# Four preln graph-attention layers on one core: the first group's query and key products made plainly and by halves, and the values of layer 3's last two groups made last

## The chip, the cores and the metric

One core of one Trainium2 chip runs the kernel. The metric is device microseconds of one execution, as the median of several; the trace shows one profiled execution. TensorE is called PE in the profile, VectorE DVE, ScalarE ACT and GpSimd POOL; SP is the engine that issues most of the DMAs, and "SPq" and "ACTq" are DMA issues on the queues of SP and ACT.

## The reference

The input is 128 graphs of 64 nodes with 512 features (8192 rows) and a 64x64 adjacency for each graph. Four layers follow, each on `h = relu(layernorm(x))` and added to `x`. All is float32. Cut to what matters:

```python
# layers 0 and 2: 4 heads of 64
q, k, v = h @ Wq, h @ Wk, h @ Wv
attn = softmax(where(adj, q @ k.T / 8, -max))
x = x + (attn @ v) @ Wo + bo
# layer 1: a second layernorm, 8 heads, the same attention with qkv and out projections
# layer 3: 8 heads
m = h @ map_w.T + map_b
n = m / norm(m per head)
cos_adj = (n @ n.T masked > 0.1)
q, k = m @ q_w.T + q_b, m @ k_w.T + k_b
adj_h = cos_adj * softmax(where(mask, NEG, q @ k.T / 8)) * keep
sem = h @ gcn_map_w.T + gcn_map_b            # the "values" of this layer
out = relu((adj_h @ sem) @ gcn_W.T / (adj_h.sum(-1) + 1))
x = x + out
```

## The kernel before

**Tiling.** The rows go in 16 groups of 512 rows (8 graphs), and the layers one after the other: group 0 to 15 of layer 0, then layer 1, and so on. A step is a pair (layer, group). For each step the rows are loaded in two halves of 256 rows (L468, on SP's queue), normalised (statistics on DVE at L433 to L438 and L442, a power on POOL at L440, the scaling on ACT at L449), transposed by PE (L500) and copied by ACT into `hT` (L505).

**Products.** A product of 512 rows with a 512x512 weight is done by a Strassen-Winograd scheme (`winograd`, L539): 7 products of quarters where a plain one has 8. Each product of quarters is 4 float32 matmuls, which the profile counts as 8 passes (`x8`). The price is sums: four of the weight's quarters, once for each weight (`sums_of_a`, L315, on POOL; kept in blocks 2, 4, 5 and 6 of the weight tile, block 2 being overwritten) and four of the input's quarters for each step (`sums_of_b`, L327, on POOL, into a tile `t`). The PSUM evictions of a product are ACT's and DVE's (L552, L556, L565, L572, L576 and, for the values of layer 3, L638 to L659). The values of layers 0 and 2 are plain products (L682, `mmv`).

**Layer 3.** For a group, `m` is made first (`map3`); then, up to group 14, the values `S2` (`sem3`, tile `v` in the profile), then q and k. In group 15 q and k come before the values. POOL adds a bias row to the values (`add_rows`, L780, four instructions), and `norms` (L791 to L827) scales `m` to unit length by way of a DRAM round trip (L811, L819, on SP's queue).

**Softmax and the end of a group.** `front` does for each half of a group's blocks (u = 0, 1): scores (L847, 64 small matmuls into the PSUM tile `sc`, of which there is one, shared with `po`), mask, maximum, subtraction (L858, L863, L866, DVE), exponential (L869, ACT), sum and reciprocal (L872, L874), scaling (L876, POOL); in layer 3 also the cosine scores from `m`, their threshold (L1108) and the mask product (L1114). The tile `E` comes from a ring of two. `last` (layer 3) transposes E (L887, copied by ACT at L891), multiplies with the values (L1141, `po`), and `finish` divides (L1052, L1054, L1057) and adds the residual (L1063). The residual rows are loaded by 16 DMAs for a group (L1042) and the result stored by 16 (L1070), all on SP's queue, and the ring `xres` of the residual tiles holds two, that is one group.

**What sets the order.** The order of the instructions on each engine is decided when the kernel is built: `Order` runs generators with estimated durations, and each one's next instruction is put down when its engine is free in that estimate. Weight loads count 10 us each there, but those that follow each other on the queue overlap, and the last one counted for `vo0` is the 2 us of `bo0`. On the chip each engine takes its instructions in that order and waits at each for what it needs. `weights` (L333 to L351) loads the weights one after the other on ACT's queue and yields the POOL sums between them:

```python
            w_ready[key].set()
            yield from sums_of_a(o_part(t) if key in ("vo0", "vo2") else t)
            w_sums[key].set()
```

Of the kernel before, what the change touches and what calls it, by code (L numbers as in the profile page):

```python
# [16 lines left out]
N = 64  # L17
# [186 lines left out]
def gnn_stack(ctx: ExitStack, tc: tile.TileContext, a: dict, out: bass.AP):  # L204
# [85 lines left out]
    def o_part(t):  # L290

        return t.rearrange("p a k n -> p (a k) n")[:, 4:11, None, :]
# [24 lines left out]
    def sums_of_b(B, T, vector=False):  # L317

        n = T.shape[2]
        for o, i0, i1 in ((T[:, 0], B(0, 1), B(0, 0)), (T[:, 1], B(1, 1), T[:, 0]),  # L320
# [4 lines left out]
            else:  # L325
                yield pool(0.65 * n)
                nc.gpsimd.tensor_tensor(o, i0, i1, ALU.subtract)  # L327

    def weights():
        for key, parts in units:  # L330
            if key == "q1":
                yield p_ready[0, 0]
            t, w_done[key] = yield from r_w.new(f"w_{key}")  # L333
            W[key] = t
            for src, dst in parts(t):
                yield ("actq", 1.0, 10.0)
                nc.scalar.dma_start(dst, src.rearrange("(c p) o -> p c o", p=P))
            if key in ("vo0", "o1", "vo2"):
                l = int(key[-1])
                src = a[f"bo{l}"]  # L340
                bo[l], bo_done[l] = yield from r_u.new(f"bo{l}")
                yield ("actq", 0.5, 2.0)
                nc.scalar.dma_start(bo[l], bass.AP(tensor=src.tensor, offset=src.offset,
                                                   ap=[[0, P], [1, D]]))
            if key in ("q1", "k1", "v1"):
                yield from gamma_into(key)
            elif key == "o1":
                yield from v_bias()
            elif key == "sem3":
                yield from gcn_fold(t)  # L350
            w_ready[key].set()  # L351
            yield from sums_of_a(o_part(t) if key in ("vo0", "vo2") else t)
            w_sums[key].set()

    bv = const.tile([P, NC], F32, name="bv")

# [93 lines left out]
                                 scale=rs[:, 0, t:t + 1])  # L450

    hT, hB, h_ready, h_done, t_done = {}, {}, {}, {}, {}

    def quarters(v):

# [32 lines left out]
    def transposes(steps):  # L488

        for l, s in steps:  # L490
            h, h_done[l, s] = yield from r_h.new("hT")
            hT[l, s] = h
            for half in range(2):
                yield n_ready[l, s, half]
                x, xe = normed.pop((l, s, half))
                for t in range(2):
                    pt, pe_ = yield from r_tr.new("ptr")
                    for c in range(NC):
                        yield pe(0.115)
                        nc.tensor.transpose(pt[:, c, :], x[:, t, c * P:(c + 1) * P], ident)  # L500
# [12 lines left out]
            yield from sums_of_b(quarters(h), T)  # L513
            sums.set()
# [67 lines left out]
    def winograd(A, BT, tokens_out, out_, used, begun):  # L582
# [102 lines left out]

    st, p_ready, s_ready, p_used, with_ones = {}, {}, {}, {}, []

    def projections(steps):
        for l, s in steps:
            yield h_ready[l, s]  # L690
            h, BT = hT[l, s], hB[l, s]
            z = st[l, s] = {}
            end = s == NG - 1
            if l in (0, 2):
                yield w_ready[f"qk{l}"]
                qk, z["qk_done"] = yield from r_qk.new("qk")
                used = yield from unit(W[f"qk{l}"], (*BT, w_sums[f"qk{l}"]), False, Out(quarters(qk)))
                od.spawn(when([used], s_ready[l, s], t_done[l, s],
                              w_done[f"qk{l}"] if end else None), 0)
                z["q"], z["k"] = qk[:, 0:2, :], qk[:, 2:4, :]  # L700
                yield w_ready[f"vo{l}"]
# [8 lines left out]
            elif l == 1:  # L710
                es = []
                for i, n in enumerate("qk"):
                    yield w_ready[f"{n}1"]
                    o, z[f"{n}_done"] = yield from r_qk.new(f"{n}T")
                    es.append((yield from unit(W[f"{n}1"], (*BT, w_sums[f"{n}1"]), False,
                                               Out(quarters(o), qkb[:, i, :]))))
                    od.spawn(when([es[-1]], w_done[f"{n}1"] if end else None), 0)
                    z[n] = o
                od.spawn(when(es[:2], s_ready[l, s]), 0)
                yield w_ready["v1"]  # L720
                V, z["v_done"] = yield from r_v.new("V")

                def vv(i, k, V=V):
                    return V[:, 2 * k:2 * k + 2, i * H:(i + 1) * H]
                es.append((yield from unit(W["v1"], (*BT, w_sums["v1"]), True, Out(vv))))
                z["v"] = V
                od.spawn(when(es, p_ready[l, s], t_done[l, s], h_done[l, s],
                              w_done["v1"] if end else None), 0)
            else:
                yield w_ready["map3"]  # L730
                mT, z["m_done"] = yield from r_m.new("mT")
                mv = quarters(mT)
                m_ready = yield from unit(W["map3"], (*BT, w_sums["map3"]), False, Out(mv, map_b))
                m_sums, z["n_ready"], m_used = od.event(), od.event(), od.event()
                od.spawn(sums_after(m_ready, mv, z, m_sums), 1)
                od.spawn(norms(mT, s, m_ready, z["n_ready"], m_used), 3)
                order = ("q", "k", "sem") if end else ("sem", "q", "k")
                es, rows = [], od.event()
                for n in order:
                    yield w_ready[f"{n}3"]  # L740
                    if n == "sem":
                        V, z["v_done"] = yield from r_v.new("S2")
                        S2 = V.rearrange("p t (h e) -> p t h e", e=N + 1)
                        if not any(V is v for v in with_ones):

                            with_ones.append(V)
                            yield pool(0.6)
                            nc.gpsimd.memset(S2[:, :, :, N:N + 1], 1.0)

                        def sv(i, k, S2=S2):  # L750
                            return S2[:, 2 * k:2 * k + 2, 4 * i:4 * i + 4, 0:N]
                        used = yield from unit(W["sem3"], (*BT, w_sums["sem3"]), True, Heads(sv))
                        od.spawn(when([m_ready, used], t_done[l, s], h_done[l, s]), 0)
                        od.spawn(add_rows(S2, used, rows), 0)
                        z["v"] = S2
# [12 lines left out]
    def sums_after(e, B, z, done):  # L768
        yield e
# [81 lines left out]
    def softmax_parts(S, se, mask, neg):  # L851

        m = mask.rearrange("p b k -> p (b k)")
        n = m.shape[1]
# [9 lines left out]
        E, e = yield from r_e.new("E")  # L864
# [12 lines left out]
        return E, e  # L877

    def transposed(E, e):

# [197 lines left out]
    def front(l, s):  # L1078
# [6 lines left out]
            z["e_ready", u] = od.event()  # L1085
        p_used[l, s].set()
        for u, blocks in enumerate(units):
            S, se = yield from scores(z["q"], z["k"], 2 * nch, blocks)
# [5 lines left out]
            E, e = yield from softmax_parts(S, se, m, (0, 1, 0, 2)[l])  # L1094
            if u == len(units) - 1:
                me.set()
            z["e", u] = E, e
# [22 lines left out]
    def last(s):  # L1120
# [102 lines left out]
```

## Time and profile before

| | |
|---|---|
| median of 6 runs | 3003.63 us (3000.38 to 3010.83) |
| profiled execution, its own time | 3004.57 us |
| its span in the profile | 3002.8 us |
| busy PE / DVE / ACT / POOL | 98% / 58% / 45% / 50% of the span |
| mean granted TensorE clock | 0.992 |
| DMA moved | 244.08 MB, 81 GB/s on average |

The page divides the span by engine, then into 40 slices, then lists DMA queues, the chain of work that ended last, and the costliest groups of instructions. A line of the timeline gives start, duration, engine, line, operation, and output and input tiles; what stands in brackets is the engine's idle time before it and what ended it. "The profile's own time" is 1.8 us above the span.

### The profile page before, as it was taken

To read this page: it belongs to the slowest core of one execution; us is meant where nothing else is said; L and a number is where in the kernel's file an instruction comes from. 1 tells how busy PE (TensorE), PEld (TensorE's weight loads), DVE (VectorE), ACT (ScalarE), POOL (GpSimd) and SP (SyncE) were. 2 spreads that over 40 slices of the span, in tenths; PEclk is the share of its full clock that TensorE was granted. 3 is DMA by queue.
4 is the path that set the end of the run, shared out by engine and by line. 5 is a ranking of instruction groups with operands and counts; after the bars stand their busy time and mean duration, and the time that the engine had idled before them with its cause. 6 is when DMAs were issued, how large, how long until landed. Compare 5 with 4: busy or idle time off the path is not lost.

```text
span 3002.8 us, 64290 instructions
## 1 busy us (share of the span) xinstructions
PE 2935.3 (98%) x27288; PEld 2490.5 (83%) x27288; DVE 1747.3 (58%) x2753; ACT 1358.4 (45%) x2489; POOL 1493.7 (50%) x1168
## 2 busy tenths in 40 slices
PE   8999999999999999999999999999999999999997
PEld 6888888888888888888888888887888877888876
DVE  5556565655555456455455646656666666665566
ACT  4444444544444444443444444454444444444442
POOL 7756666634434434435566656663344443344332
PEclk9999999999999999999999999999999999999998
DMA  4332423211111111212323232332223222222112
GB/s 133 118 112 87 123 93 123 82 44 66 65 44 66 65 44 60 71 44 80 110 87 130 87 123 94 123 95 62 69 80 90 69 62 62 70 87 71 51 48 62
DMA packets 162960, 244.08 MB, mean 81 GB/s; under 512 B 17393, under 2 KB 69617, under 8 KB 162673
## 3 DMA queue, kind: packets, MB, share of 16 engines
q1 hardware_dynamic: 149760, 226.56, 24.0%
q10 hardware_dynamic: 12912, 13.42, 1.5%
q8 instruction: 214, 3.51, 0.5%
q14 instruction: 74, 0.60, 0.1%
HBM read 168.60 MB, written 71.30 MB: 80 GB/s over the span
## 4 chain that ended last, share of the span: by engine, by line
PE 87%; DVE 4%; ACT 4%; DMA 2%; POOL 2%; issue 1%; SPq 0%; DVEq 0%; POOLq 0%; ACTq 0%
PE mA L539 37%; PE mC L539 19%; PE mB L539 10%; PE mmv L682 5%; PE sc L847 5%; PE ptr L500 4%; PE ptp L887 3%; PE po L1006 2%; PE po L1141 1%; ACT E L869 1%; DVE sc L858 1%; PE mmn L796 1%; DVE E L866 1%; DVE mx L863 1%; ACT m L556 1%
## 5 line engine op out<-in xcount | busy, mean ns | idle before, releaser
L931 POOL TENSOR_TENSOR xres<-xres,u 128x512 f32<-128x512 f32 x192 | 252.9, 1338 | 351.4 <-DMA xres<-x 158.4
L433 DVE BATCH_NORM_STATS2 st<-xin 128x6 f32<-128x512 f32 x320 | 215.7, 674 | 317.2 <-DMA xin<-x 252.4
L876 POOL TENSOR_TENSOR E<-E,sm 128x1024 f32<-128x1024 f32 x96 | 186.5, 1943 | 419.4 <-DVE sm L874 297.4
L952 POOL TENSOR_TENSOR xres<-xres,u 128x512 f32<-128x512 f32 x192 | 243.9, 1271 | 244.2 <-ACT u L947 238.8
L449 ACT ACTIVATE xin<-xin,rs 128x512 f32<-128x512 f32 x320 | 243.7, 808 | 105.5 <-DVE rs L442 105.4
L682 PE MATMUL mmv<-w_vo,hT 128*128 128x256 f32 x1024 | 236.9, 384 | 1.1 <-DVE xres L565 1.1
L440 POOL TENSOR_TENSOR rs<-rs,mhalf 128x2 f32<-128x2 f32 x160 | 119.4, 746 | 232.4 <-DVE rs L438 201.5
L682 PEld LDWEIGHTS mmv<-w_vo,hT 128*128 128x128 f32 x1024 | 195.3, 192 | 30.2 <-DVE xres L565 3.0
L327 POOL TENSOR_TENSOR t<-hT 128x512 f32<-128x512 f32 x128 | 185.8, 1452 | 40.4 <-ACT hT L505 40.3
L442 DVE SCALAR_TENSOR_TENSOR rs<-mv,rs 128x2 f32<-128x2 f32 x160 | 73.6, 460 | 198.8 <-POOL rs L440 198.7
L539 PE MATMUL mA<-t,w_q 128*128 128x256 f32 x768 | 188.9, 382 | 0.0
L539 PE MATMUL mA<-t,w_k 128*128 128x256 f32 x768 | 183.7, 381 | 4.8 <-ACT kT L556 4.7
L539 PE MATMUL mA<-t,w_qk 128*128 128x256 f32 x768 | 187.3, 380 | 0.4 <-POOL t L327 0.4
L505 ACT COPY hT<-ptr 128x512 f32<-128x512 f32 x256 | 151.7, 593 | 76.5 <-PE ptr L500 76.5
L327 POOL TENSOR_TENSOR t<-hT,t 128x512 f32<-128x512 f32 x128 | 177.4, 1386 | 4.9
L500 PE MATMUL ptr<-ident,xin 128*128 128x128 f32 x1024 | 159.8, 279 | 13.6 <-ACT xin L449 13.6
L539 PEld LDWEIGHTS mA<-t,w_k 128*128 128x128 f32 x768 | 145.4, 191 | 28.4 <-ACT kT L556 8.0
L891 ACT COPY pt<-ptp 128x512 f32<-128x512 f32 x192 | 112.6, 587 | 110.3 <-PE ptp L887 110.3
L539 PEld LDWEIGHTS mA<-t,w_qk 128*128 128x128 f32 x768 | 143.8, 191 | 19.4 <-POOL t L327 0.8
L539 PEld LDWEIGHTS mA<-t,w_q 128*128 128x128 f32 x768 | 142.3, 190 | 18.4
L872 DVE TENSOR_REDUCE sm<-E 128x16 f32<-128x1024 f32 x96 | 116.4, 1212 | 69.4 <-ACT E L869 69.3
L780 POOL TENSOR_TENSOR v<-v,gcn_row 128x512 f32<-128x512 f32 x64 | 81.4, 1306 | 150.4 <-ACT v L638 150.4
(222 smaller groups left out, 6830.6 us busy)
## 6 DMA issues: line engine op xcount, KB each, us to landing
x<-xres SPq DMA_DIRECT2D x96, 512.0 KB, 3.9
xin<-x SPq DMA_DIRECT2D x96, 512.0 KB, 3.7
xres<-x SPq DMA_DIRECT2D x64, 512.0 KB, 4.4
xin<-in_x SPq DMA_DIRECT2D x32, 512.0 KB, 3.9
xres<-in_x SPq DMA_DIRECT2D x32, 512.0 KB, 4.7
u<-rs SPq DMA_DIRECT2D x128, 128.0 KB, 3.2
xres<-x SPq DMA_DIRECT2D x256, 64.0 KB, 2.3
out<-xres SPq DMA_DIRECT2D x256, 64.0 KB, 2.1
```

Of the source, the lines that this page charges most:

```text
L327: nc.gpsimd.tensor_tensor(o, i0, i1, ALU.subtract)
L433: nc.vector.bn_stats(st, v[:, t, :])
L440: nc.gpsimd.tensor_tensor(rs[:, 0, :], rs[:, 1, :], mhalf[:, :2], ALU.pow)
L449: nc.scalar.activation(v[:, t, :], v[:, t, :], func, bias=rs[:, 2, t:t + 1], scale=rs[:, 0, t:t + 1])
L500: nc.tensor.transpose(pt[:, c, :], x[:, t, c * P:(c + 1) * P], ident)
L505: nc.scalar.copy(h[:, :, b * P:(b + 1) * P], pt)
L539: nc.tensor.matmul(o, l, r, start=(first and m == 0 and k == 0), stop=(k == KC - 1), skip_group_check=True)
L682: nc.tensor.matmul(p_[:, 0:n], inT[:, c, t * P:(t + 1) * P], w[:, c, :], start=(c == 0), stop=(c == NC - 1))
L847: nc.tensor.matmul(S[a_ * N:(a_ + 1) * N, par, col], lT[r, c, k], rT[r, c, k], start=True, stop=True)
L876: nc.gpsimd.tensor_mul(E, E, sm[:, :, None].to_broadcast([P, 16, N]))
L931: nc.gpsimd.tensor_add(xr[:, t, :], xr[:, t, :], bo[l])
L952: nc.gpsimd.tensor_add(v, v, both(u))
```

## The change

1. **First group.** `transposes` announces the first half of layer 0's group 0 when its two blocks of `hT` are there (`h_half`), and makes no input sums for this group. `projections` takes this group's q and k with a new `plain` instead of `winograd`: for each half of the tokens (k = 0, 1) and for q and k (i = 0, 1) two products of quarters, 8 in all.
2. **Weight sums.** The four sums of `Wq0`/`Wk0` are taken out of the row of weight loads into a generator of their own, which starts when the plain products are done (they read the quarters that the sums overwrite).
3. **Layer 3, groups 14 and 15.** Their values are put into a list, and made after group 15's q and k: group 14's, then group 15's. The order "q, k, values" held for group 15 alone before.
4. **Softmax.** `E` is taken before the scores; for the last half of the last group it is a tile of the ring of q and k. `attentions` no longer waits for the values before it transposes E in layer 3; `last` does so after the transposes.

```diff
+    def sums(key, A, after=None):
+        if after is not None:
+            yield after
+        yield from sums_of_a(A)
+        w_sums[key].set()
...
             w_ready[key].set()
-            yield from sums_of_a(o_part(t) if key in ("vo0", "vo2") else t)
-            w_sums[key].set()
+            if key == "qk0":
+                od.spawn(sums(key, t, plain_done), 4)
+            else:
+                yield from sums(key, o_part(t) if key in ("vo0", "vo2") else t)
...
+                if (l, s, half) == (0, 0, 0):
+                    hT[l, s] = h
+                    h_half.set()
+            if (l, s) == (0, 0):
+                hB[l, s] = quarters(h), None
+                h_ready[l, s].set()
+                continue
...
+    def plain(A, h, out_, used):
+        B = quarters(h)
+        es = []
+        for k in range(2):
+            if k:
+                yield h_ready[0, 0]
+            for i in range(2):
+                p_, e = yield from (r_ma if i else r_mm).new("mP")
+                yield from product(p_, A[:, 2 * i], B(0, k), False, True)
+                yield from product(p_, A[:, 2 * i + 1], B(1, k), False, False)
+                od.spawn(out_.alone(i, k, p_, e), 0)
+                es.append(e)
+        od.spawn(when(es, used), 0)
...
-                order = ("q", "k", "sem") if end else ("sem", "q", "k")
+                late = s >= NG - 2
                 es, rows = [], od.event()
-                for n in order:
+                if late:
+                    behind.append((s, z, BT, m_ready, rows))
+                for n in ("q", "k") if late else ("sem", "q", "k"):
...
+                if end:
+                    for b in behind:
+                        yield from sem(*b)
...
         for u, blocks in enumerate(units):
+            if (l, s, u) == (3, NG - 1, 1):
+                E, e = yield from r_qk.new("E")
+                E = E.rearrange("p c t -> p (c t)")[:, 0:16 * N].rearrange("p (i k) -> p i k", k=N)
+            else:
+                E, e = yield from r_e.new("E")
             S, se = yield from scores(z["q"], z["k"], 2 * nch, blocks)
...
             pt, pte = yield from transposed(*z["e", u])
+            yield p_ready[3, s]
...
             yield p_used[l, s]
-            yield p_ready[l, s]
+            if l < 3:
+                yield p_ready[l, s]
```

More of the change, by code (lines that the diff above doesn't have):

```diff
@@ L452, in gnn_stack @@
     hT, hB, h_ready, h_done, t_done = {}, {}, {}, {}, {}
+    h_half, plain_done = od.event(), od.event()
     def quarters(v):
@@ L686, in gnn_stack, with sem @@
     st, p_ready, s_ready, p_used, with_ones = {}, {}, {}, {}, []
+    behind = []
+    def sem(s, z, BT, m_ready, rows):
+        yield w_ready["sem3"]
+        V, z["v_done"] = yield from r_v.new("S2")
+        S2 = V.rearrange("p t (h e) -> p t h e", e=N + 1)
+        if not any(V is v for v in with_ones):
+            with_ones.append(V)
+            yield pool(0.6)
+            nc.gpsimd.memset(S2[:, :, :, N:N + 1], 1.0)
+        used = yield from unit(W["sem3"], (*BT, w_sums["sem3"]), True, Heads(
+            lambda i, k: S2[:, 2 * k:2 * k + 2, 4 * i:4 * i + 4, 0:N]))
+        od.spawn(when([m_ready, used], t_done[3, s], h_done[3, s]), 0)
+        od.spawn(add_rows(S2, used, rows), 0)
+        z["v"] = S2
     def projections(steps):
         for l, s in steps:
-            yield h_ready[l, s]
-            h, BT = hT[l, s], hB[l, s]
+            yield h_half if (l, s) == (0, 0) else h_ready[l, s]
+            h = hT[l, s]
+            if (l, s) != (0, 0):
+                BT = hB[l, s]
             z = st[l, s] = {}
@@ L696, in projections @@
                 qk, z["qk_done"] = yield from r_qk.new("qk")
-                used = yield from unit(W[f"qk{l}"], (*BT, w_sums[f"qk{l}"]), False, Out(quarters(qk)))
-                od.spawn(when([used], s_ready[l, s], t_done[l, s],
+                if (l, s) == (0, 0):
+                    used = plain_done
+                    yield from plain(W["qk0"], h, Out(quarters(qk)), used)
+                else:
+                    used = yield from unit(W[f"qk{l}"], (*BT, w_sums[f"qk{l}"]), False,
+                                           Out(quarters(qk)))
+                od.spawn(when([used], s_ready[l, s], t_done.get((l, s)),
                               w_done[f"qk{l}"] if end else None), 0)
@@ L736, in projections @@
                 od.spawn(norms(mT, s, m_ready, z["n_ready"], m_used), 3)
-                order = ("q", "k", "sem") if end else ("sem", "q", "k")
+                late = s >= NG - 2
                 es, rows = [], od.event()
-                for n in order:
+                if late:
+                    behind.append((s, z, BT, m_ready, rows))
+                for n in ("q", "k") if late else ("sem", "q", "k"):
                     yield w_ready[f"{n}3"]
                     if n == "sem":
[L742 to L755, printed above, removed]
+                        yield from sem(s, z, BT, m_ready, rows)
                         continue
@@ L849, in scores, with softmax_parts @@
         return S, e
-    def softmax_parts(S, se, mask, neg):
+    def softmax_parts(S, se, E, mask, neg):
         m = mask.rearrange("p b k -> p (b k)")
@@ L863, in softmax_parts @@
         nc.vector.tensor_reduce(mx, S3, AX.X, ALU.max)
-        E, e = yield from r_e.new("E")
         yield dve(1.2)
@@ L1087, in front @@
         for u, blocks in enumerate(units):
+            if (l, s, u) == (3, NG - 1, 1):
+                E, e = yield from r_qk.new("E")
+                E = E.rearrange("p c t -> p (c t)")[:, 0:16 * N].rearrange("p (i k) -> p i k", k=N)
+            else:
+                E, e = yield from r_e.new("E")
             S, se = yield from scores(z["q"], z["k"], 2 * nch, blocks)
@@ L1093, in front @@
             m = mask[:, blocks[0]:blocks[0] + len(blocks)]
-            E, e = yield from softmax_parts(S, se, m, (0, 1, 0, 2)[l])
+            yield from softmax_parts(S, se, E, m, (0, 1, 0, 2)[l])
             if u == len(units) - 1:
```

1 line of the change is left out of this document (removed).

## The prediction

> **What bounds the kernel now.** I read the page's busy times first, then the waits of PE, then the timeline of the two ends, since PE leaves room nowhere else.
>
> ```profile
> PE 2935.3 (98%) x27288; PEld 2490.5 (83%) x27288; DVE 1747.3 (58%) x2753; ACT 1358.4 (45%) x2489; POOL 1493.7 (50%) x1168
> ```
>
> PE idles 67.5 us of 3002.8. By the windows, 14.0 lie in the first 50 us and 17.6 in the last 33 (below: window, length, then busy PE, PEld, DVE, ACT, POOL, granted clock, DMA share, GB/s). The change touches the two ends, so about 30 us is all there is to win.
>
> ```profile
> 2970.00:2980.00 10.00, 7.26 (x152) 5.78 (x152) 9.76 (x10) 1.20 (x4) 6.36 (x4) 1.00 0.01 4
> 2980.00:2990.00 10.00, 4.29 (x128) 3.87 (x128) 6.93 (x10) 2.02 (x3) 3.95 (x3) 0.62 0.12 26
> 2990.00:3003.00 13.00, 3.88 (x80) 2.93 (x75) 5.51 (x13) 1.17 (x2) 0.00 (x0) 0.63 0.29 62
> ```
>
> The timeline of the start, POOL and PE:
>
> ```profile
> 10.65 0.69 POOL L440 TENSOR_TENSOR rs<-rs,mhalf 128x2 f32<-128x2 f32 x1 [2.09 <-DVE rs L438]
> 12.97 3.97 POOL L315 TENSOR_TENSOR w_qk<-w_qk 128x512 f32<-128x512 f32 x3 [1.63 <-DMA w_qk<-in_Wk]
> 23.14 0.70 POOL L440 TENSOR_TENSOR rs<-rs,mhalf 128x2 f32<-128x2 f32 x1
> 24.94 0.66 PE L500 MATMUL ptr<-ident,xin 128*128 128x128 f32 x4 [2.52 <-ACT xin L449]
> 26.98 3.03 POOL L315 TENSOR_TENSOR w_vo<-w_vo 128x256 f32<-128x256 f32 x4 [0.35 <-DMA w_vo<-in_Wo]
> ```
>
> The power of each half's normalisation (L440) stands in POOL's order between sums; at 24.94 PE waits for one that came after nine sums.
>
> **Start.** What goes: group 0's input sums (4 of 1.27 us on POOL) and the waits of PE for them (0.42 and 2.52). What comes: an eighth product, 8 passes of 0.2157 = 1.73 us of PE. PE may begin with half 0 when `hT` has it (12.25) and not at 14.78. But the built order shows what else moves. Since the `w_qk` sums no longer hold up the row of weight loads, the four DMAs of `w_vo` and `bo0` now stand on ACT's queue ahead of the table load and the first normalisation, and the four `w_vo` sums stand on POOL ahead of the power for half 1 of group 0.
>
> ACT first: its last moved DMA waits for the second `xin` (issued 1.6, landed 6.9 later, 8.5), another for `bdw` (8.2). Two issues of 0.46, then the table load of 1.28, give 10.4 where the first normalisation began at 8.79: half 0 is 1.66 later, its transposes at 11.3, its copies done at 13.9.
>
> POOL next: the first `w_vo` sum reads the second half of `Wo`, which lies behind `Wk` and `Wv` on the queue.
>
> ```profile
> w_qk<-in_Wk ACTq DMA_DIRECT2D x1, 512.0 KB, 10.0
> ```
>
> `Wk`, issued at 2.91, landed at 12.9, with the DMA engines full: 372 GB/s on average from 7 to 11.4. Everything that is ahead of it now was ahead before. `Wv` and the two halves of `Wo` are 1.05 MB more; at 372 GB/s they land at 12.9 + 2.8 = 15.7. Four sums of 0.757 end at 18.8, the power at 19.5, DVE's step at 19.7, the first ACT row at 20.5, and PE transposes half 1 at 20.6, against 13.01 before. Half 0's two products (16 passes, at half clock until about 16.3 as before, so 18.6 to 20.3) fill most of that wait. From 20.6 PE has until the first product of group 1: 6 sets of transposes at 0.44, 48 passes of 0.2157 (10.36), and the values with one set of scores between (8.2, before from 32.96 to 41.16). That is 21.2, so 41.8 against 41.16: **+0.7 us**. Bounds: if half 0 ran on without a wait from 12.3, 38.9 (-2.2); if `Wo` lands behind everything and a second clock window stays halved, +2.4. I take +0.7, as the landing rests on measured bytes. The moved `w_qk` sums (POOL, about 39.8 to 45.1) delay the scaling of E to 47.0, where PE asks for it at 46.6; the fourth sum is wanted later. From there the order regains its old one within some 80 us, and after that it is the same up to group 14 of layer 3.
>
> **Layer 3, group 14.** The reference point is 2859.08: second scores of group 13, when the threshold (2857.81 + 1.23) frees the bank `sc`. Before, the values' matmuls filled such waits. The new order from here through q and k is that of group 15 before (2920.74 to 2959.78), with its SP order too: the adjacency load behind the round trip of the norms.
>
> ```profile
> 2947.52 0.43 DVE L907 TENSOR_SCALAR nz<-adj 128x512 uint8<-128x512 uint8 x1 [6.61 <-DMA adj<-in_adj]
> 2950.46 0.70 PE L1141 MATMUL po<-v,pt 64*64 64x65 f32 x32 [2.29 <-DVE y L1057]
> 2951.08 3.15 PE L539 MATMUL mC<-t,w_k 128*128 128x256 f32 x8
> ```
>
> DVE stands 6.61 us at that load, PE 2.29 for DVE, and then 8 passes take 3.15 and not 1.73. So group 14 ends at 2859.08 + 39.04 = 2898.1. Group 15's `map3` and its next scores take 15.95 as before (2904.79 to 2920.74): 2914.1. Norms and transposes 4.74: 2918.8. Then q and k with one set of scores and no `po`: 112 passes of 0.2157, 1.09 and 0.33 = 25.6: 2944.4 (the adjacency is ahead of the round trip here, so no stall). Group 14's values with two scores: 15.3 (2959.78 to 2975.06 before): 2959.7. Group 15's 17 matmuls ahead of the first `po`, with scores: 8.8, and DVE's subtraction, 2.2 of mask while POOL adds rows, ends at 2968.9. All products are done near 2976, before at 2975.1: the values now fill PE's waits on the last softmax, but the stall of group 15 came back in group 14.
>
> One rule can be set against this. After 2.29 us without work the granted clock was 0.83 from 2950 to 2960; after 2.52 us at 24.94 it stayed 1.00. The Trainium skill, TensorE: Matmul & The Clock Gate, "Why this matters for your kernels", asks for no gap over some 3 us; by it group 14's gap keeps the full clock, and the end would fall 1.4 earlier. The sum goes by the row 3.15.
>
> **The end, on SP's queue.** This decides. The stores of group 14 cannot start before `po` of group 14 and DVE's four steps: 2968.9 + 0.7 + 1.1 + 0.7 = about 2971.6. Behind them stand 16 residual loads of group 15 (their tiles are freed by those stores) and its 16 stores.
>
> ```profile
> 2956.07 11.19 SPq L1042 DMA_DIRECT2D xres<-x  x16
> 2986.53 13.89 SPq L1070 DMA_DIRECT2D out<-xres  x16
> L1070 SPq DMA_DIRECT2D out<-xres x256: 466/594/1790, 2037.3 to 2999.8; - x128
> DMA to landing us min/median/max: 1.9/2.1/4.8
> ```
>
> Before, those loads were through by 2967. Now 48 issues of 0.60 (the median; loads 0.595) come after 2971.6. Step by step: stores of blocks 0 and 1 of group 14 from 2971.6 and 2975.4, block 2 from 2978.9 to 2981.3; two loads, then block 3 to 2984.9; six loads to 2988.5; two of the second tile to 2989.7. Block 0 of group 15 has its rows at 2987.8 (2.3 to land), so DVE's add ends at 2988.5 though `po` was ready near 2985; DVE stands in order, so the later blocks wait too. Stores to 2992.1, two loads to 2993.3, stores of block 1 to 2995.7, four loads to 2998.1, landed at 2999.8. Stores of block 2 to 3000.5, DVE's add for block 3 at 3000.5, its stores to 3002.9, the last landing 2.1 after its issue at 3002.3, and the 0.87 that the span ran on after it before: 3005.3. Against 3002.8 that is **+2.5**. Without the loads in the way, PE and DVE alone would end at 2992.6 + 5.3 = 2997.9.
>
> **Sum.** +0.7 + 2.5 = +3.2 on the profiled execution's own 3004.57: 3007.8. The median lies 0.94 below that execution: **3006.8**.
>
> **The rivals.**
> - Both ends as the change says: half 0 runs on from 12.3 (-2.2) and group 15's rows are there when DVE asks (-4.9): 3003.6 - 7.1 = 2996.5. For it: PE's idle 17.6 us at the end. Against it: the built orders of POOL and SP. Chance 0.07.
> - Slower by more: SP's price. The 16 loads at 2956.07 took 0.70 each, not 0.60. At 0.70 the 48 issues cost 4.8 more: 3011.6. It passes +6.0 from 0.66 an issue on. For it: stores and loads alternate now, each held to landings. Against it: the medians over 256 issues of each. Chance 0.21.
> - Nothing to see: issues near their least (0.466) take 6 off the queue, PE's order binds again and the end is as before or 1 us earlier: 3003. Chance 0.12.
> - The forecast, a small loss: 0.60.
>
> **Range and chances.** About 0.2%, 6.0 us, is what a measurement of this kernel tells from no change. Low: 3006.8 less 2.9 (start at its lower bound), 1.4 (8 passes in 1.73 and not 3.15) and 3.2 (the lowest run lies that far below the median) is 2999.3; high: plus 4.8 (SP) and 1.7 (start) is 3013.3. The first rival is left out. Faster by over 0.2%: 0.07, the first rival. Slower: 0.21 and 0.03 of the forecast's upper end, 0.24. Within: 0.69.
>
> **What would show it.** At the start: POOL's `w_vo` sums at about 15.7 ahead of L440's second power, and half 1's transposes near 20.6. At group 14: DVE waiting for the adjacency and PE some 2 us for `po`. At the end: SP issuing without pause from about 2975, DVE's residual adds of group 15 ended by DMA, PE done near 2995. It is wrong if those adds wait for `po` alone, or if PE's first product of group 1 starts before 40 or after 44.

## The result and the profile after

The changed kernel is slower: 3014.82 us (median of 24 runs, 3008.40 to 3020.03) beside 3005.0 for the kernel before in the same job, a ratio of 1.0032 [1.0026, 1.0039]. The forecast was 3006.8, with a range up to 3013.3: the sign was right, the loss is 9.6 us and not 3.2, and the time lies outside the range. (Of the 8.0 us between 3006.8 and 3014.82, 1.4 are the base: the forecast added to 3003.63, the median of 6 runs, and the 48 runs beside the changed kernel have 3005.0.) The profiled execution took 3020.03, the longest of the 24, with a span of 3018.2; a second one, below, has 3008.5.

The page of the changed kernel, and its windows over the last 33 us (length, busy PE, PEld, DVE, ACT, POOL, granted clock, DMA share, GB/s):

```profile
PE 2938.3 (97%) x27296; PEld 2489.9 (82%) x27296; DVE 1736.7 (58%) x2750; ACT 1356.1 (45%) x2488; POOL 1490.8 (49%) x1164
```

```profile
2985.00:2995.00 10.00, 5.86 (x169) 4.76 (x168) 8.38 (x13) 1.82 (x4) 7.21 (x5) 0.83 0.35 80
2995.00:3005.00 10.00, 4.74 (x104) 3.97 (x104) 3.68 (x9) 1.17 (x2) 0.00 (x0) 0.56 0.36 89
3005.00:3018.00 13.00, 0.00 (x0) 0.00 (x0) 2.36 (x5) 0.00 (x0) 0.00 (x0) 0.50 0.40 96
```

PE is busy for 3 us more than before. Its last product now ends nearly 14 us ahead of the span's end; DVE has 2.36 us to do in the last 13. What ends last is none of these engines.

The start, from the timeline of POOL and PE:

```profile
15.71 3.01 POOL L315 TENSOR_TENSOR w_vo<-w_vo 128x256 f32<-128x256 f32 x4 [7.30 <-DMA w_vo<-in_Wo]
18.68 0.71 POOL L448 TENSOR_TENSOR rs<-rs,mhalf 128x2 f32<-128x2 f32 x1
20.48 0.66 PE L509 MATMUL ptr<-ident,xin 128*128 128x128 f32 x4
...
41.73 1.46 PE L556 MATMUL mA<-hT,w_qk 128*128 128x256 f32 x6
```

POOL stands 7.30 us before the `w_vo` sums, with the power for half 1 behind them, and the first product of group 1 begins 0.73 later than the 41.00 of before: all as the sum had it. (Its 41.16 is the end of the matmul before that product.)

Group 14 of layer 3 (SP, DVE and PE in the timeline):

```profile
2890.63 0.59 SPq L948 DMA_DIRECT2D adj<-in_adj  x1
2893.50 0.43 DVE L955 TENSOR_SCALAR nz<-adj 128x512 uint8<-128x512 uint8 x1 [6.36 <-DMA adj<-in_adj]
2896.44 0.70 PE L1196 MATMUL po<-v,pt 64*64 64x65 f32 x32 [2.04 <-DVE y L1105]
2897.07 3.63 PE L556 MATMUL mC<-t,w_k 128*128 128x256 f32 x8
```

The stall that group 15 had is in group 14 now, nearly to the number: 6.36 for DVE, 2.04 for PE, and the 8 passes behind it at half speed.

The end: SP's queue from the first store of group 14 on, then the residual adds of DVE.

```profile
2980.35 10.50 SPq L1118 DMA_DIRECT2D out<-xres  x12
2991.02 1.64 SPq L1090 DMA_DIRECT2D xres<-x  x2
2992.71 2.51 SPq L1118 DMA_DIRECT2D out<-xres  x4
2995.57 4.95 SPq L1090 DMA_DIRECT2D xres<-x  x8
3000.61 3.77 SPq L1118 DMA_DIRECT2D out<-xres  x4
3004.43 1.23 SPq L1090 DMA_DIRECT2D xres<-x  x2
3005.76 2.46 SPq L1118 DMA_DIRECT2D out<-xres  x4
3008.26 2.51 SPq L1090 DMA_DIRECT2D xres<-x  x4
3010.87 5.01 SPq L1118 DMA_DIRECT2D out<-xres  x8
```

```profile
2998.90 0.69 DVE L1111 SCALAR_TENSOR_TENSOR xres<-y,xres 128x512 f32<-128x512 f32 x1 [3.64 <-DMA xres<-x]
3001.24 0.69 DVE L1111 SCALAR_TENSOR_TENSOR xres<-y,xres 128x512 f32<-128x512 f32 x1 [0.61 <-DMA xres<-x]
3007.57 0.69 DVE L1111 SCALAR_TENSOR_TENSOR xres<-y,xres 128x512 f32<-128x512 f32 x1 [4.46 <-DMA out<-xres]
3012.64 0.69 DVE L1111 SCALAR_TENSOR_TENSOR xres<-y,xres 128x512 f32<-128x512 f32 x1 [3.34 <-DMA xres<-x]
```

Loads and stores alternate as foreseen, from 2988.4 on with no pause of SP over 0.34, and all four adds of group 15 end a wait on DMA. (The third names a store as its releaser; its rows were issued from 3004.43 on, 0.6 apiece, and landed 2.3 later.)

**Splitting the difference by a mark.** As reference I take the last `w_map` products of group 14, the last ones ahead of what the second part reorders. In the first pair of profiles the mark went from 2857.67 to 2865.56, 7.9 later, and the stretch from the mark to the end of the span from 145.1 to 152.6, 7.5 longer. The forecast had 0.7 and 2.5. Two theories came out of that: the middle, 7.2 of it unforeseen, is scatter and the end costs more than was summed; or the shifted start costs something all the way.

### The profile page after: what moved, and what is told of

The parts are those of the page before. It is cut to its first block, busy times and chain, and to the rows that moved or that the text cites. A ratio compares the mean times of both kernels' runs of the same rounds, so it can differ in the third digit from the quotient of the medians.

```text
span 3018.2 us, 64289 instructions
## 1 busy us (share of the span) xinstructions
PE 2938.3 (97%) x27296; PEld 2489.9 (82%) x27296; DVE 1736.7 (58%) x2750; ACT 1356.1 (45%) x2488; POOL 1490.8 (49%) x1164
## 4 chain that ended last, share of the span: by engine, by line
PE 84%; DVE 5%; ACT 4%; DMA 2%; POOL 2%; issue 1%; SPq 1%; DVEq 0%; POOLq 0%; ACTq 0%
PE mA L556 36%; PE mC L556 18%; PE mB L556 10%; PE sc L897 4%; PE mmv L714 4%; PE ptr L509 4%; PE ptp L935 3%; PE po L1054 2%; ACT E L918 1%; PE po L1196 1%; DVE sc L908 1%; DVE E L915 1%; DVE mx L913 1%; PE mmn L846 1%; ACT m L573 1%
## 5 line engine op out<-in xcount | busy, mean ns | idle before, releaser
L556 PEld LDWEIGHTS mA<-t,w_k 128*128 128x128 f32 x768 | 145.1, 190 | 29.7 <-ACT kT L573 9.6
L556 PEld LDWEIGHTS mA<-t,w_qk 128*128 128x128 f32 x744 | 139.7, 191 | 18.2 <-ACT qk L569 0.3
```

The lines of the kernel that those rows point to most:

```text
L556: nc.tensor.matmul(o, l, r, start=(first and m == 0 and k == 0), stop=(k == KC - 1), skip_group_check=True)
```

## The experiments

The ratios are to the kernel before, run on the same chip. All marks and ends stand here in one table (us; "end" is the span less the mark; "start" is where the first product of group 1 begins). The last column is the stall by the adjacency, in group 15 in the order of before and in group 14 in the new one: how long PE waited for DVE ahead of the second `po`, and whether the passes behind that start 0.216 us apart ("full") or some 0.427 ("half", for 4 to 8 passes).

| kernel | ratio | start | mark | end | stall |
|---|---|---|---|---|---|
| before, first profile | | 41.00 | 2857.67 | 145.1 | 2.29, half |
| before, second profile | 0.9997 [0.9985, 1.0010] | 40.98 | 2857.43 | 143.3 | 1.80, full |
| changed, first profile | 1.0032 [1.0026, 1.0039] | 41.73 | 2865.56 | 152.6 | 2.04, half |
| changed, second profile | 1.0031 [1.0021, 1.0040] | 42.26 | 2857.70 | 150.8 | 1.83, full |
| start alone | 1.0008 [0.9999, 1.0016] | 41.80 | 2860.92 | 143.2 | 1.72, full |
| second part alone | 1.0028 [1.0017, 1.0039] | 41.41 | 2861.61 | 150.9 | 1.94, full |
| changed, residual rows early | 1.0004 [0.9996, 1.0013] | 42.15 | 2860.15 | 142.2 | 2.04, full |
| the same, adjacency early | 0.9998 [0.9987, 1.0008] | 41.81 | 2859.16 | 139.8 | none |
| second part alone, both early | 0.9989 [0.9979, 0.9999] | 42.47 | 2855.92 | 139.7 | none |
| changed, merged loads and stores | 1.0038 [1.0026, 1.0050] | 41.67 | 2862.95 | 151.9 | 1.88, full |
| changed, the second merging | 1.0040 [1.0025, 1.0055] | 42.07 | 2858.19 | 152.6 | 2.23, half |
| changed, group 15's loads merged | 1.0027 [1.0018, 1.0037] | 41.75 | 2860.59 | 146.7 | 2.08, full |
| changed, `vo0` later | 1.0021 [1.0013, 1.0030] | 39.25 | 2855.72 | 153.4 | 3.29, half |
| changed, all three | 0.9977 [0.9967, 0.9987] | 38.57 | 2853.25 | 139.3 | none |
| all three and the first merging | 0.9994 [0.9986, 1.0003] | 39.57 | 2857.48 | 142.8 | none |
| all three and the second merging | 0.9989 [0.9979, 0.9999] | 38.56 | 2854.07 | 142.6 | none |

**The changed kernel again.** No edit.

> The changed kernel, a second time. Two places are to be told apart: the stretch between the first group's products and the last of group 14's projections (the mark: the last four w_map products before the group's q and k), which came 7.9 us later in the changed kernel's profile than in that of before, with 0.6 us of it there already at 41 us; and the end behind the mark, which is another 7.5 us longer. Theory A (the 7 us of the middle are mostly scatter between executions, since the profiled execution, 3020.0, was the longest of its 24, 5.2 above their median): this profile has the mark within 3 us of before's 2857.7, while its end behind the mark is again 151 to 154 us long, against 145.1 before. Rival B (the shifted start costs something in every execution): the mark is at 2863 to 2867 again. Median either way 3013 to 3016.

Measured: the mark at 2857.70, the end 150.8, median 3011.61. Theory A holds on the mark; its end missed the lower bound of 151 by 0.2, and the median lies below the 3013 to 3016 that both theories had. The 7 us of the middle were one execution's. The variant with the second part alone, whose order up to the mark is that of before, shows the same: its mark is at 2861.61, and 2855.92 in its later form. One profile fixes the mark to some 4 us either way, no better.

**The start alone.** The kernel before with the first part of the diff.

> The kernel before with the first part of the change alone: the first group's products plain and by halves, without its difference tiles, and the sums of w_qk behind them; layer 3 as before. From about the 75th group of matrix products on, the order of every engine is that of before. Theory A: the start costs 0.6 us, what comes behind nothing: 3004 to 3007 beside 3005, a ratio of 1.0000 to 1.0005. Rival B: the shift of the start sets the middle back as well, 5 to 8 us: a ratio of 1.0017 to 1.0026, and the first product's shift at 41 us is still 0.6.

Measured: 3005.67, a ratio of 1.0008 [0.9999, 1.0016]; the ratio lies between the two ranges, the time in A's, and the interval shuts out all of B's ratios. The start costs 0.8 at 41 us and nothing that can be seen behind.

**The second part alone.** The kernel before with the second part of the diff.

> The kernel before with the second part alone: the values of groups 14 and 15 of layer 3 come last, with E of the last softmax in a buffer of q and k; the start as before. Theory A: the end carries nearly all of the loss: 7 to 9.5 us above before, a ratio of 1.0023 to 1.0032. Rival B: the end costs what was forecast, 2.5 us, a ratio of 1.0005 to 1.0012, and the rest is in the start and the middle.

Measured: 3012.65, 1.0028 [1.0017, 1.0039], 8.4 us, and 150.9 behind the mark. So the loss is the second part's, as theory A says.

**Group 15's residual rows out of the way.** The ring `xin` has tiles of the same shape, free in layer 3 once group 15 is transposed:

```diff
-                v2, e2 = yield from r_xres.new()
+                v2, e2 = yield from (r_xin if s == NG - 1 else r_xres).new()
...
+        if s == NG - 2:
+            ahead.append({(n, t): od.event() for t in range(TB) for n in ("e", "out")})
+            od.spawn(last_residuals(NG - 1, ahead[0]), 2)
```

> The changed kernel, but the residual rows of group 15 go to two buffers of the input ring, which layer 3 no longer needs by then, and their 16 loads are issued with those of group 14, ahead of all stores: none of the last adds waits on a load behind a store in SP's queue. Theory Q (that queue is what made the end 5 us longer than forecast): the last stores are bound by the last matrix products and by 32 issues at 0.62 us from 2980 on, which end at 3000; the end is 5 to 12 us earlier than the changed kernel's, 3003 to 3010. Rival P (the end is set by TensorE at half clock and by its small products, done at 3004.4): within 2 us of the changed kernel, with the waits on loads gone and others in their place.

Measured: 3004.53, 1.0004 [0.9996, 1.0013], against 1.0031 for the changed kernel on the same chip: 8 us back. SP's queue in this variant:

```profile
2897.18 10.18 SPq L1090 DMA_DIRECT2D xres<-x  x16
2907.40 11.30 SPq L1090 DMA_DIRECT2D xin<-x  x16
...
2973.25 13.24 SPq L1118 DMA_DIRECT2D out<-xres  x16
2988.91 11.08 SPq L1118 DMA_DIRECT2D out<-xin  x16
```

The waits of DVE near the end (us in total, times, longest), of the changed kernel's second profile and then of this variant:

```profile
DVE xres L1111 <- DMA xres<-x: 8.8, 3, 4.7
DVE xres L1111 <- DMA out<-xres: 4.0, 1, 4.0
DVE f L1100 <- PE po L1196: 2.4, 2, 1.3
```

```profile
DVE f L1100 <- PE po L1204: 4.3, 5, 1.6
DVE Cf L1162 <- PE sc L897: 0.5, 1, 0.5
```

All loads are issued by 2918.7. The 12.8 us that DVE waited for DMA are gone, and it waits for PE, as it should. The 16 stores of group 15 still run on SP without waiting for an add once the first is there (11.08, 0.69 each), so the row of issues ends last here too, but it is 16 long and not 40. Theory Q holds; rival P, that PE sets the end, does not.

**Fewer issues, three attempts.** If the length of SP's queue is what counts, fewer and larger DMAs should do as well without a new buffer. The first makes 2 DMAs of 64x2x256 of each 4, loads and stores:

```diff
+            for s2 in range(2 if s >= NG - 2 else 0):
+                nc.sync.dma_start(xr[s2 * N:(s2 + 1) * N], two(x_of(3, s), t * P, s2))
...
+        for s2 in range(2 if s >= NG - 2 else 0):
+            nc.sync.dma_start(two(out, row, s2), xr[s2 * N:(s2 + 1) * N])
```

> The changed kernel, with the residual loads and the stores of groups 14 and 15 as 8 DMAs of 64x2x256 for a group in place of 16 of 64x256, the same bytes in the same places and in the same order: 24 issues at the end in place of 48. Theory N (SP's queue costs by the issue, 0.67 us for each of the last 36 in the second profile of the changed kernel, whatever an issue moves): 24 issues less are up to 16 us off the queue, so it no longer sets the end, what remains are the landings: 5 to 9 us below the changed kernel, a ratio to before of 1.0000 to 1.0015. Rival B (the cost goes by bytes): an issue takes about 1.2 to 1.3, the queue is as long as it was, within 2 us of the changed kernel, 1.0025 or more.

Measured: 1.0038 [1.0026, 1.0050], 3016.58. Theory N's time is missed; rival B's time is what came, but not its price. The line of its stores on SP (duration of an issue in ns, min/median/max) and SP's waits over the last 55 us:

```profile
L1125 SPq DMA_DIRECT2D out<-xres x16: 595/596/642, 2975.9 to 3011.5; - x16
```

```profile
SPq L1125 <- DMA out<-xres: 14.9, 8, 2.1
SPq L1094 <- DMA out<-xres: 3.5, 1, 3.5
```

An issue of twice the bytes costs what the smaller one cost, 0.596, so theory N is right on the price. But the two stores of a block now interleave in the output, the second was made to wait for the landing of the first, eight times, and these waits ate what the issues saved. The second attempt keeps the stores of a block apart (one of 128x256 and two of 64x256):

```diff
+        if s >= NG - 2:
+            nc.sync.dma_start(out[row:row + N, :].rearrange("p (s e) -> s p e", s=2), xr[:, 0, :])
```

> The changed kernel again with fewer issues for groups 14 and 15, cut so that no two stores of a block interleave in the output: 8 loads of 64x2x256 for a group in place of 16, and 3 stores for a block (one of 128x256 for its first 64 rows, two of 64x256) in place of 4. From the first store of group 14 on that is 32 issues in place of 48, the same bytes, the same buffers, the same order. In the first such attempt a store waited 2.1 us for the landing of the one before it, while an issue itself took 0.60 for twice the bytes. Theory N (the queue costs by the issue): 16 issues less take about 10 us off the queue, the residual rows come before po asks for them, and the time is 6 to 10 us below the changed kernel's, a ratio to before of 0.9998 to 1.0013. Rival L (what counts is the order, a load behind a store behind an add, with landings of 2 to 3 us, not the number of issues): less than 4 us below the changed kernel, 1.0018 or more, and the adds of group 15 still end their waits on DMA.

Measured: 1.0040 [1.0025, 1.0055], so theory N's time is missed, and L's is what came. No store waits for another now, but the 64x256 stores, which landed in 2.1 before, have this line (landing in us, min/median/max), and a load of group 15 stood 3.8 behind one. The trace has the landing of only two of these 16 stores, 4.4 and 6.1:

```profile
DMA to landing us min/median/max: 4.4/5.3/6.1
```

```profile
SPq L1094 <- DMA out<-xres: 3.8, 1, 3.8
```

The span ends 5.9 us behind the last issue (3004.9 to 3010.8), where it was 2.4 in the changed kernel; that last landing is the better evidence. Among the stores the larger one in front is what is new; why it should hold up the landing of the others is not shown. The third attempt leaves all stores alone and merges only the loads of group 15.

> The changed kernel with only the residual loads of group 15 cut to 8 of 64x2x256; all stores as in the changed kernel, so none of the larger stores whose landing took 5 us. From the first store of group 14 on that is 40 issues in place of 48; in the built order the loads of the second tile now stand ahead of all stores of group 15, behind one wait for the landing of group 14's last stores. Theory N (the row of issues sets the end): 8 issues at 0.67 less the wait of about 1: the last store is issued 4 to 6 us earlier behind the mark than in the changed kernel, a ratio to before of 1.0010 to 1.0020. Rival L (only the order of loads behind stores counts): within 2 us of the changed kernel, 1.0025 or more, with adds of group 15 still waiting on DMA for 3 us or more each.

Measured: the end is 146.7 behind the mark and the last issue 144.4, against 150.8 and 148.4: the last issue is 4.0 earlier, the lower edge of N's 4 to 6. The time, 1.0027 [1.0018, 1.0037] beside the changed kernel's 1.0031 [1.0021, 1.0040] in another job, cannot tell that from nothing, and its point is L's. So the number of issues does count in the trace, at some 0.5 each; in the two attempts before, waits for landings and a late last landing took that gain.

**The adjacency of group 14 early.** On top of the variant with early residual rows; the only change in any engine's order is one DMA on SP.

```diff
+        if (l, s) == (3, NG - 3):
+            od.spawn(adj_ahead(NG - 2), 2)
```

> The variant with group 15's residual rows in two buffers of the input ring, and one DMA moved besides: the adjacency of group 14 is issued ahead of the residual stores and loads of group 12 or 13 and of the round trip of group 14's norms, not behind them. It tells what the stall in group 14's iteration costs. Theory S (the stall costs what its rows show): PE's wait of 2.0 for y and the 8 passes at 3.6 in place of 1.7 go, the stretch from the mark (the last w_map products of group 14) to the first po of group 14 falls from 110.4 to 106 to 108, and the time is 2 to 4 us below that variant. Rival R (the wait is replaced by the next, of DVE or of ACT behind the norms): the stretch stays at 109 to 111 and the time within 1.5 us.

Measured: 3002.24, 2.3 below that variant's 3004.53 (other chip), with 0.9998 [0.9987, 1.0008]; the intervals of the two ratios overlap. From the mark to the first `po` of group 14 it takes 108.4 where it took 110.4, and the end 139.8 where it was 142.2. The timeline at the same place, first of the variant without this move, then with it:

```profile
2891.03 0.70 PE L1204 MATMUL po<-v,pt 64*64 64x65 f32 x32 [2.04 <-DVE y L1105]
2891.65 1.99 PE L556 MATMUL mC<-t,w_k 128*128 128x256 f32 x8
```

```profile
2880.67 0.42 DVE L969 TENSOR_SCALAR nz<-adj 128x512 uint8<-128x512 uint8 x1
...
2887.94 0.70 PE L1220 MATMUL po<-v,pt 64*64 64x65 f32 x32
...
2888.56 1.99 PE L556 MATMUL mC<-t,w_k 128*128 128x256 f32 x8
```

No bracket is left behind any of the three. The 8 passes take 1.99 in both: the variant without the move has the same wait of 2.04 as the changed kernel's first profile, but not its half speed, so the 2.0 us are the wait alone. That is why theory S, which counted the slow passes as well, holds in kind and just misses its 106 to 108. The stretch is the firm evidence: the five profiles with this move have 108.3 to 108.4, the eight of the new order without it 110.2 to 110.5 at full speed and 112.1 to 113.2 at half.

**`vo0` later.** The changed kernel, with one line in `weights`:

```diff
+            if key == "vo0":
+                yield n_ready[0, 0, 1]
             t, w_done[key] = yield from r_w.new(f"w_{key}")
```

> The changed kernel, with the weight row vo0 held back until the normalisation of group 0's second half has been put down, so that neither its DMA issues on ACT's queue nor its sums on POOL stand ahead of group 0's powers and scalings. Theory T (those two queues are what the start lost): half 1 is transposed near 13 to 14 and not at 20.5, and the first product of group 1 begins at 38 to 39.5 in place of 41.7 to 42.3, 2 to 4 us below the changed kernel, the end being as in the changed kernel. Rival U (PE's halved clock and the later landing of Wv and Wo take its place): the first product of group 1 at 41 or later.

Measured: 3010.45, 1.0021 [1.0013, 1.0030], 3 us below the changed kernel's ratio. The start:

```profile
10.44 0.69 POOL L450 TENSOR_TENSOR rs<-rs,mhalf 128x2 f32<-128x2 f32 x1 [2.14 <-DVE rs L448]
14.76 1.06 PE L511 MATMUL ptr<-ident,xin 128*128 128x128 f32 x4
...
19.34 1.54 POOL L315 TENSOR_TENSOR w_vo<-w_vo 128x256 f32<-128x256 f32 x2 [5.42 <-DMA w_vo<-in_Wo]
...
39.25 1.46 PE L558 MATMUL mA<-hT,w_qk 128*128 128x256 f32 x6
```

The power for half 1 comes at 10.44, not 18.68, and its transposes at 14.76, later than the 13 to 14 expected but 5.7 ahead of 20.48. Group 1 starts at 39.25: 2.5 earlier than with the change, 1.7 earlier than before. Theory T.

**Together.** First with the first merging of DMAs in it, in an earlier job:

> All of it together: the change, with group 15's residual rows in free buffers, 8 DMAs in place of 16 for groups 14 and 15, the adjacency of group 14 early, and the weight row vo0 behind group 0's normalisation. If the parts add up (the end at 142 behind the mark less 2.3 for the shorter row of last stores and 3 for the stall, the start 2 to 4 earlier): 2995 to 2999, a ratio to before of 0.997 to 0.9985. If the parts only hide each other: 3001 to 3004, no difference.

It gave 0.9994 [0.9986, 1.0003] and 3002.70, in the range for parts that hide each other: the interleaved stores took back 3.5 us of the end (142.8 behind the mark, not 139.3). Then without merging, and with the second merging:

> The change with three things beside it: group 15's residual rows in two buffers of the input ring, the adjacency of group 14 early, the weight row vo0 behind group 0's normalisation. If the parts add up, 2.5 to 3 us below the variant without the last part (3002.2): 2999 to 3000, a ratio to before of 0.9980 to 0.9992. If they do not: as that variant, 0.9998.

> The former, with 8 loads and 12 stores for groups 14 and 15 in place of 16 and 16. By the issue's price the last block's stores come 0.6 earlier and the row of stores ahead of them is 4 issues shorter: 1 to 3 us below the former, 2996 to 2999, a ratio to before of 0.9970 to 0.9985. If the last adds and landings set the end now: within 1 us of the former.

Measured: 2997.56, 0.9977 [0.9967, 0.9987] without, 3001.73, 0.9989 [0.9979, 0.9999] with it. The parts add up, to a little more than expected; this version beats both kernels. The merged stores lose some 4 us again, where a gain or no change was expected.

**What the base was, and what the second part is worth.** Two runs more.

> The kernel before, for a second profile. The forecast added its 2.5 us to one execution of it, whose end behind the mark (group 14's last w_map products) took 145.1; the variant with the start alone has the same order there and took 143.2. Theory B (that base was some 2 us long): 142.5 to 144 behind the mark. Rival C (145 is usual, and the second part costs 5.7 to 7.5 there): 144.6 to 145.6.

Measured: 143.3, theory B. The execution that the forecast was added to had an end 1.8 us longer than this one and the start variant's 143.2. The difference lies at the stall: a wait longer by 0.5 and passes at half speed behind it in that execution, at full speed in the other two.

> The second part of the change alone, the start as before, with group 15's residual rows in two free buffers of the input ring and the adjacency of group 14 early. It tells what the later values are worth once nothing stands behind a store. Theory V (they fill PE's waits for the last softmax): 139 to 140.5 behind the mark, 3 to 5 us below before, a ratio of 0.9983 to 0.9993. Rival W (the reordering only moves the waits, and it was the load queue alone that differed): 142.5 to 145 behind the mark and 1.0000, so that the gain of the best variant comes from the start.

Measured: 3000.75, 0.9989 [0.9979, 0.9999] and 139.7, theory V. Its end is 3.6 us below that of before. The wait of 5.16 us that PE had for ACT ahead of group 15's first `po` is gone, so the values made last do fill it, and shorter waits for DVE come in its place. Not all of the 3.6 is theirs: with the residual rows early and the stall left in, the end is 142.2, some 1.0 below before, and the other 2.4 came with the adjacency. Whether the kernel before would gain as much from an early adjacency of its group 15 was not run.

## Why the prediction was wrong, by its own steps

**Start, +0.7: right, as far as single profiles show it.** The sums stood at 15.71 (15.7 forecast), half 1's transposes at 20.48 (20.6), group 1's first product at 41.73 (41.8). In the table the changed start lies between 41.67 and 42.26, that of before between 40.98 and 42.47. The cause it named, the weight row on POOL's and ACT's queues, is shown by the run that moves that row: 39.25, and 38.57 with the other moves, beside the 38.9 of the favourable bound.

**The middle, nothing: right**, though the first pair of profiles said +7.2. The marks of the table spread from 2853 to 2866, and two variants whose order is that of before up to the mark have 2855.92 and 2861.61.

**Group 14: the stall right, its half speed a matter of luck.** The wait of PE for DVE behind the adjacency stands in all eight profiles of the new order that leave that load where it is. The slow passes behind it do not: the sum copied the row 3.15 from one execution, and the two other profiles with the order of before have their passes at full speed. In the changed kernel's first profile the granted clock was 0.86 over the 10 us from 2890, in the second 1.00 over the same stretch (from 2882 there). The first `po` of group 14 was forecast 111.2 behind the mark and came at 112.1 with the slow passes and at 110.2 without. Here the Trainium skill (TensorE: Matmul & The Clock Gate, "Why this matters for your kernels") asks for no gap of PE over some 3 us, so that the clock does not fall. Of the ten waits under 3 us in the table, seven left the clock at full speed, as that rule has it, and three (2.04, 2.23 and 2.29) were followed by half speed: a gap below 3 us is no safe one here. A wait of 2.04 stands on both sides, so its length alone does not decide; what does is not shown.

**The end: the mechanism right, the term "48 issues at 0.60" too small.** This is the step that failed. From the first store of group 14 to the end of the span the sum had 33.7 (2971.6 to 3005.3). Measured are 37.9 in both profiles. Nearly all of that lies in the row that the prediction itself called decisive: from the end of the third block's add to the last issue there are 40 issues, forecast at 24.0 (2978.9 to 3002.9), measured 27.4 (2988.44 to 3015.88), which is 0.686 each. The other 0.8 is ahead of that add. The median issue is 0.595, just as the row of before said. But that is the duration of an issue, and issue by issue the trace shows 0.044 us between the end of one and the start of the next, so that they start 0.639 apart even where SP waits for nothing. Those gaps make 1.7 of the missing 3.4; seven longer ones, of 0.10 to 0.34, make 0.7; and two issues of 1.1 to 1.9 lift the sum of the durations by 1.0. The second profile splits in the same way. The row 11.19 for 16 loads, 0.70 each, stood among the quoted lines and held all of this, since it too is a closed row of issues, and it was left to the second rival. That rival, "slower by more: SP's price", given 0.21 and said to pass +6.0 from 0.66 an issue on, had nearly the right price. Its reason, loads and stores that alternate, covers at most the longer gaps.

**The pieces, like with like.** The end was counted from one execution, 145.1 behind the mark, with the slow passes in it. With them the end went from 145.1 to 152.6, without them from 143.3 to 150.8: 7.5 us both times, where the sum had 2.5. Of the 5.0 it lacked with the slow passes, 4.2 came from the first store on, and 0.9 ahead of it, where the first `po` came at 112.1 and not 111.2. Added up with the start: 0.7 + 2.5 + 4.2 + 0.9 = 8.3, where the ratio says 9.6 [7.8, 11.7].

**The other rivals.** "Nothing to see" needed issues at their least, 0.466; they were not. The first rival, both ends as the change says, was priced at -7.1; with the three moves of DMAs it was built, and 0.9977 is -6.9. Its condition was not met by the change as written, and that its price came out is in part luck: the early adjacency, 2.4 us at the end, was not in it, and for the residual rows, which it had at -4.9 from 145.1, the run with these alone shows 142.2 against 143.2 and 143.3. "PE and DVE alone would end at 2997.9" is 140.2 behind the mark, with group 14's stall in it; the run that has this stall and the rows early took 142.2, 2.0 more. That the run without the stall has 139.7 does not confirm that sum.

**DMA, row and rule.** The 64x256 store landed a median 2.1 us behind its issue. The Trainium skill (DMA: Bandwidth & Descriptors, "Anatomy of one DMA", which describes the GpSimd path) puts the fixed cost of some 2 us mostly to waiting for the write to be confirmed, not to set-up. The duration of the landing agrees. In the closed row these landings overlap, and only the last is paid; what set the end is the 0.64 to 0.69 of SP's own time for each issue, which comes one after the other.

## What to carry to other kernels

When work is moved to the end, follow what its buffers let go: here the values filled PE's waits, and the loads of the next rows slid behind the stores that free their tiles; tiles from a ring that was already idle, and DMAs issued earlier, turned a loss of 8 us into a gain of 3. A queue without slack is priced by a closed row of its issues, from start to start, not by the median duration of one; merging DMAs makes the row shorter but can buy waits for landings instead. A row that is copied from one execution can hold something, here passes at half speed, that most others do not have. And before a difference of a few us is given to a stretch of the program, a second profile of the same kernel should say how much that stretch moves by itself.

## What the runs showed of the hardware that was not expected

- An issue on SP's queue costs the same for 64 KB and 128 KB: 0.595 and 0.596 at the median. With the 0.044 between two issues, 64 KB ones start 0.639 apart.
- Where 64x256 stores share a block with one 128x256 store, the span ended 5.9 and 5.8 us behind the last issue in two runs, where it was 2.4 among their like, and the two landings on record took 4.4 and 6.1, not 2.1. The cause stays open.
- Single issues on a busy queue take 1.1 to 1.9 us, two to three times the median. What holds those few is not shown either.
- After a wait of PE of 1.7 to 2.3 us its next passes ran at half speed in three profiles of ten.
